# Slot tables of a graph kernel with the kind of slot outermost and the range of nodes innermost

## The chip, the cores and the metric

The kernel runs on one core of one Trainium2 chip. The metric is the device time of one execution, in microseconds. The core has a matrix engine (TensorE, PE, with a separate path PEld for loading weights), a vector engine (VectorE, DVE), a scalar engine (ScalarE, ACT), a general engine (GpSimd, POOL) and an engine that issues DMAs (SyncE, SP). DMAs are issued from SP, ACT and POOL and run on 16 DMA engines. Two kinds of memory lie on the chip: SBUF, with 128 partitions, and PSUM, into which PE writes. What is called DRAM below is the chip's large memory.

## The reference

Two layers run over the same graph of N = 32,768 nodes with 128 features and E = 524,288 directed edges (src to dst, sorted by dst).

```python
# layer 0
agg = segment_sum(x[src], dst, N)
h_local = bn(x + mlp((1 + eps) * x + agg))
h_attn = bn(x + attention(x))          # 64 blocks of 512 nodes, 8 heads
h = h_local + h_attn
x = layernorm(x + bn(h + mlp2(h)))
# layer 1, three times
attn = softmax((x @ Wq.T + bq) @ keys.T)    # 512 keys
lap = x - dinv * segment_sum(dinv[dst] * x[dst], src, N)
x = 0.5 * x + 0.5 * (attn @ values - 0.2 * lap)
# then two layer norms and a residual
```

So four sums over edges are computed: one that gathers by src and adds at dst, and three that gather by dst and add at src.

## The kernel before, in words

Nodes are cut into 256 windows of 128. An edge belongs to a pair of windows, one of its source and one of its target. The first KS = 6 edges of a pair get a regular slot; further edges of a window come in OW = 5 lists of 128, and what is left is shared by eight windows in SH = 2 lists. A window therefore has NC2 = 2 * 6 + 5 + 2 = 19 kinds of slot with 128 lanes each.

A sum over edges has two halves. In the first, `spread` multiplies the rows of a window of nodes by a pick matrix and stores the result to DRAM (`slots`), so that it can be read back by the receiving window. In the second, `Sums` fetches for each window those rows (`y_i`), gathers the 5 lists and at times the 2 shared ones with indirect DMAs on POOL (L1431), builds a one-hot matrix `oh` of 128 x 19 x 128 on DVE (`hot`, L1442), and lets PE add 19 products up in PSUM (`add`, L1455). The one-hot compares a ramp 1 to 128 with the slot table: for window i, 19 numbers per lane, each repeated over 128 columns.

The tables (slot, other, shared and row, each for "dst" and "src") depend on the edges alone and are built by the kernel itself while the attention of layer 0 runs. `prologue` is a generator: it sorts edges on DVE, moves words to their slots, transposes with PE through one PSUM bank (`turned`, L516 and L517, a copy by ACT out of that bank) and stores tables to DRAM. `attention_steps` is a list of steps written out by hand, and the last part of the program gives the generator a quota of time between steps (SHARE = 3.35 us for each place). A yield of WAIT skips places while a DMA is under way; BANK asks for a place where the PSUM bank `m`, which attention also uses, is free. The order is fixed this way, and each engine runs its own instructions in that order.

`build` handles two halves h of 128 windows each. At its end it issues on SP, in this order: the slot table of dst (L794), row of dst (L796), the regular slots of src from the tile `half` (L802), row of src (L807). The tiles of a half lie in pools that are given up and used again: `word`, in which the next half sorts (L148), lies where these tiles were. `build_more` then sorts the left-over edges: it loads `more_a` on SP (L816), first used by DVE at L236, and at its end stores the remaining 7 kinds of slot of src (L873), then other (L875) and shared (L876). Attention's own load of the next block (`xa`, L1543, read by PE at L1546) and its result (`attn_d`, L1674) go out on SP too, between these.

After attention: the spread of layer 0 (from 3,785 us), its collecting (from 4,790, when L1347 loads the slot table of dst), the MLP (6,840 to 7,075), the first spread of layer 1 (the slot table of src is loaded at 7,075), then twice collecting and spreading together (8,552 to 13,290), and the last collecting (to the end).

Before the change the slot tables have the window outermost and the 19 kinds innermost, on the chip `[128, windows, 19]` and in DRAM `(w c)`, in bfloat16.

Of the kernel before, what the change touches and what calls it, by code (L numbers as in the profile page):

```python
# [11 lines left out]
BF16 = mybir.dt.bfloat16  # L12
FP8 = mybir.dt.float8e4
AF = mybir.ActivationFunctionType
OP = mybir.AluOpType
# [4 lines left out]
P = 128  # L20
# [9 lines left out]
KS = 6  # L30
OV = 6
OW = 5
GW = 8
SH = 2
# [377 lines left out]
class Grid:  # L412
# [130 lines left out]
    def build(self, pp):  # L543
# [9 lines left out]
        with tc.tile_pool(name="gr", bufs=1) as sp:  # L553
# [13 lines left out]
            for h in range(2):  # L567
                with tc.tile_pool(name=f"gr_h{h}", bufs=1) as hp:
# [87 lines left out]
                            yield from left(over_w, 2 << b)  # L656

                    with tc.tile_pool(name=f"gr_c{h}", bufs=1) as ap:
                        slot = ap.tile([P, P, NC2], BF16, name="slot")
                        other = ap.tile([P, P, OW], I32, name="other")  # L660
                        shared = ap.tile([P, P // GW, SH], I32, name="shared")
                        keys = ap.tile([P, P], F32, name="keys")
# [14 lines left out]
                        yield one / 3  # L677
                        for t, n in ((0, 3), (3, OW - 3)):
                            yield from self.turned(pp, [fb[:, (t + j) * P:(t + j + 1) * P] for j in range(n)],
                                        slot[:, :, 2 * KS + t:2 * KS + t + n].rearrange("e w t -> e t w"))  # L680
                        nc.vector.tensor_copy(keys, fb[:, OW * P:OL])
                        yield two / 3
                        key = moved[:, :OL]
# [12 lines left out]
                        for t, n in ((0, 3), (3, OW - 3)):  # L696
                            yield from self.turned(pp, [fb[:, (t + j) * P:(t + j + 1) * P] for j in range(n)],
                                        other[:, :, t:t + n].rearrange("e w t -> e t w"))
                        yield from self.share(pp, ap, keys, fb[:, OW * P:OL], n_over, self.bad[:, at + h:at + h + 1],
                                   slot[:, :, 2 * KS + OW:].rearrange("e w t -> e t w"), shared)  # L700
                        nc.sync.dma_start(mine["shared"][:, h * P // GW * SH:(h + 1) * P // GW * SH],
                                          shared.rearrange("p g t -> p (g t)"))
                        nc.sync.dma_start(mine["other"][:, h * P * OW:(h + 1) * P * OW],
# [85 lines left out]
                        for g in range(2):  # L789
                            for r in range(0, KS, 3):  # L790
                                yield from self.turned(pp, [va[:, g, r + j, :] for j in range(3)],
                                            slot[:, :, g * KS + r:g * KS + r + 3].rearrange("d w r -> d r w"))
                                yield from self.turned(pp, [vb[:, g, r + j, :] for j in range(3)], row[:, g, r:r + 3, :])
                        nc.sync.dma_start(mine["slot"][:, h * P * NC2:(h + 1) * P * NC2],  # L794
                                          slot.rearrange("p w c -> p (w c)"))
                        nc.sync.dma_start(  # L796
                            mine["row"].rearrange("p (g h f) -> p g h f", g=2, h=2)[:, :, h, :],
                            row.rearrange("p g r w -> p g (r w)"))

                        half = ap.tile([P, NW, KS], BF16, name="half")  # L800
                        nc.scalar.copy(half.rearrange("p w r -> p (w r)"), fb)
                        nc.sync.dma_start(  # L802
                            theirs["slot"].rearrange("p (w c) -> p w c", c=NC2)[:, :, h * KS:(h + 1) * KS],
                            half)
                        row2 = ap.tile([P, 2, KS, P], BF16, name="row2")
                        nc.scalar.copy(row2, va)
                        nc.sync.dma_start(theirs["row"][:, h * Q:(h + 1) * Q],  # L807
# [1 line left out]

    def build_more(self, lane, pp):  # L810

        tc, nc, NC2, OL = self.tc, self.tc.nc, self.NC2, self.OL
        over = self.over
        with tc.tile_pool(name="mo_s", bufs=1) as sp:
            t = sp.tile([P, over.F], F32, name="more_a")
            nc.sync.dma_start(t.bitcast(I32), self.more.rearrange("p h f -> p (h f)"))  # L816
            spare = sp.tile([P, over.F], F32, name="more_b")
            yield WAIT
            yield from over.sort(sp, pp, t, spare, lane, (over.F // 2).bit_length() - 1)
        yield WAIT  # L820
        yield from over.find_windows(pp)
        L = OL + P
        with tc.tile_pool(name="mo", bufs=1) as sp:
            slot = sp.tile([P, 2, P, OW + SH], BF16, name="slot")
            other = sp.tile([P, 2, P, OW], I32, name="other")
            shared = sp.tile([P, 2, P // GW, SH], I32, name="shared")
            keys = sp.tile([P, P], F32, name="keys")
            words = []
            for h in range(2):
                words.append(sp.tile([P, L], I32, name=f"word{h}"))  # L830
                nc.gpsimd.indirect_dma_start(out=words[h], out_offset=None, in_=over.table,
                                             in_offset=bass.IndirectOffsetOnAxis(ap=over.at[:, h:h + 1], axis=0))
            yield 8 * WAIT
            for h in range(2):
                word = words[h]
                m = sp.tile([P, L], I32, name="m")
                n = sp.tile([P, L], I32, name="n")
                valid = sp.tile([P, L], F32, name="valid")
                val = sp.tile([P, L], F32, name="val")
                sz = sp.tile([P, 1], F32, name="sz")  # L840
                w = sp.tile([P, 1], F32, name="w")
                nc.vector.tensor_scalar(w, over.lane_f, float(h * P + 2), None, op0=OP.add)
                nc.vector.tensor_scalar(m, word, over.WSHIFT, None, op0=OP.logical_shift_right)
                yield L / 1000
                nc.vector.tensor_scalar(valid, m, w, None, op0=OP.is_equal, op1=OP.add, accum_out=sz)
                yield L / 1000
                nc.vector.tensor_scalar(self.bad[:, 4 + h:5 + h], sz, float(OL), None, op0=OP.is_gt)
                nc.vector.tensor_scalar(m, word, over.own, P - 1, op0=OP.logical_shift_right, op1=OP.bitwise_and)
                yield L / 1000
                nc.vector.scalar_tensor_tensor(val, m, 1.0, valid, op0=OP.add, op1=OP.mult)  # L850
                yield L / 1000
                for t, c in ((0, 3), (3, OW - 3)):
                    yield from self.turned(pp, [val[:, (t + j) * P:(t + j + 1) * P] for j in range(c)],
                                slot[:, h, :, t:t + c].rearrange("e w t -> e t w"))
                nc.vector.tensor_copy(keys, val[:, OW * P:OL])
                yield L / 1000
                nc.vector.tensor_scalar(m, word, over.OSHIFT, 2 * P - 1, op0=OP.logical_shift_right,
                                        op1=OP.bitwise_and)
                yield L / 1000
                nc.vector.tensor_scalar(m, m, 7, None, op0=OP.logical_shift_left)  # L860
                yield L / 1000
                nc.vector.tensor_scalar(n, word, over.oth, P - 1, op0=OP.logical_shift_right, op1=OP.bitwise_and)
                yield L / 1000
                nc.vector.tensor_tensor(m, m, n, OP.bitwise_or)
                yield L / 1000
                nc.vector.tensor_tensor(val, m, valid, OP.mult)
                yield L / 1000
                for t, c in ((0, 3), (3, OW - 3)):
                    yield from self.turned(pp, [val[:, (t + j) * P:(t + j + 1) * P] for j in range(c)],
                                other[:, h, :, t:t + c].rearrange("e w t -> e t w"))  # L870
                yield from self.share(pp, sp, keys, val[:, OW * P:OL], sz, self.bad[:, self.NBAD - 2 + h:self.NBAD - 1 + h],
                           slot[:, h, :, OW:].rearrange("e w t -> e t w"), shared[:, h])
            nc.sync.dma_start(self.out["src"]["slot"].rearrange("p (w c) -> p w c", c=NC2)[:, :, 2 * KS:],  # L873
                              slot.rearrange("p h w t -> p (h w) t"))
            nc.sync.dma_start(self.out["src"]["other"], other.rearrange("p h w t -> p (h w t)"))  # L875
            nc.sync.dma_start(self.out["src"]["shared"], shared.rearrange("p h g t -> p (h g t)"))  # L876

# [14 lines left out]
def tile_gnn_resnorm(ctx: ExitStack, tc: tile.TileContext, a: dict, out: bass.AP):  # L892
# [68 lines left out]
    w = {}  # L961
# [366 lines left out]
    class Exchange:  # L1328
# [14 lines left out]
            nc.sync.dma_start(self.row.rearrange("p h f -> p (h f)"), self.grid["row"])  # L1343

        def load_tables(self, pool):
            self.slot = pool.tile([P, NW, NC2], BF16, name="slot")
            nc.sync.dma_start(self.slot.rearrange("p w c -> p (w c)"), self.grid["slot"])  # L1347
            self.other = pool.tile([P, NW, OW], I32, name="other")
            nc.scalar.dma_start(self.other.rearrange("p w c -> p (w c)"), self.grid["other"])
            self.shared = pool.tile([P, NW // GW, SH], I32, name="shared")  # L1350
            nc.scalar.dma_start(self.shared.rearrange("p g c -> p (g c)"), self.grid["shared"])
# [88 lines left out]
        def hot(self, wp, i, ramp, bufs):  # L1440
            oh = wp.tile([P, NC2, P], BF16, name="oh", bufs=bufs)
            nc.vector.tensor_tensor(oh, ramp[:, None, :].to_broadcast([P, NC2, P]),  # L1442
                                    self.slot[:, i, :].unsqueeze(2).to_broadcast([P, NC2, P]), OP.is_equal)
            return oh

        def add(self, ps, oh, got, k):
# [733 lines left out]
```

## Time and profile before

| | us |
|---|---|
| Median of 3 runs | 14,449.62 (14,442.07 to 14,455.55) |
| The profiled execution: its own time | 15,348.34 |
| Its span, first to last instruction | 15,346.2 |
| PE busy | 12,388.1 (81%) |
| DVE busy | 11,407.8 (74%) |
| ACT busy | 6,684.1 (44%) |
| POOL busy | 6,062.4 (40%) |
| One-hots L1442, 1,024 of them | 2,745.6 |

The mean clock granted to PE was 0.90 of full speed. The DMA engines moved 3,603 MB in 1,733,387 packets, of which 292,786 were under 512 bytes. A busy share is an average over stages that have different limits, so a stage is read by its own waits. A line of the waits reads: engine, tile and line that waited, what it waited for, total us, times, longest us. A line of the groups reads: line, engine, operation, output and inputs with shapes, count, busy us and mean ns of one, then idle time before it and what ended it. A timeline line has start, length, engine, line, operation, output and input, count, and in brackets idle time before it. "SPq" is SP's queue of DMA issues: its length is the time of issuing, and not that of the transfer.

### The profile page before, as it was taken

The numbers are of one execution on the slowest core, as the hardware profiler recorded it, in microseconds if no ns is written. First come the engines' busy times: TensorE is split into PE (matmuls) and PEld (weight loads), VectorE is DVE, ScalarE is ACT, GpSimd is POOL, SyncE is SP. The second block draws the span as 40 slices with busy tenths as digits, with TensorE's granted clock in tenths as the row PEclk, the third lists the DMA queues.
The fourth block names the chain that finished last, engine by engine and source line by source line (L and its number), as shares of the span: only waits on it lengthen the run. The fifth ranks groups of instructions, "written<-read, shape, count | busy, mean of one in ns | idle before, by whom it ended". The sixth has DMA issues, their size and how long they took to land. (4 is left out here: it accounts for less than half of the span.)

```text
span 15346.2 us, 168164 instructions
## 1 busy us (share of the span) xinstructions
PE 12388.1 (81%) x58980; PEld 5857.4 (38%) x58982; DVE 11407.8 (74%) x16677; ACT 6684.1 (44%) x10316; POOL 6062.4 (40%) x5461
## 2 busy tenths in 40 slices
PE   8886897887886777779999798989798888755555
PEld 3222232232333333334444354444454444422222
DVE  7986996775997777777888676767566666577777
ACT  4343333334994000017888455555455555500000
POOL 0000000000003666640000577777577777566665
PEclk9887887888998888889999999999999999977777
DMA  1004004005998888877888899999899999877776
GB/s 38 10 11 13 10 10 13 13 16 50 349 347 296 259 262 263 263 228 248 304 311 308 304 367 356 364 360 361 303 366 360 359 360 361 324 250 250 248 252 223
DMA packets 1733387, 3602.99 MB, mean 235 GB/s; under 512 B 292786, under 2 KB 1069906, under 8 KB 1731378
## 3 DMA queue, kind: packets, MB, share of 16 engines
q1 hardware_dynamic: 1258736, 2936.81, 55.2%
q0 software_dynamic: 258752, 533.02, 11.8%
q10 hardware_dynamic: 215042, 122.32, 2.6%
q8 instruction: 465, 7.62, 0.2%
q14 instruction: 392, 3.21, 0.1%
HBM read 2088.45 MB, written 1503.00 MB: 234 GB/s over the span
## 5 line engine op out<-in xcount | busy, mean ns | idle before, releaser
L1431 POOL DMA_INDIRECT listed<-rows,other x5120 | 5688.1, 1111 | 4426.1 <-issue 3237.7
L1418 ACT CAST y_o<-exp 128x768 bf16<-128x768 f32 x4224 | 3238.7, 808 | 1365.2 <-PE exp L1413 867.0
L1413 PE MATMUL exp<-rows,pick 128*128 128x384 bf16 x12288 | 2784.6, 327 | 514.8 <-ACT y_o L1418 234.5
L1455 PEld LDWEIGHTS <-oh 128*128 128x128 bf16 x19456 | 2011.7, 104 | 2954.9 <-issue 1849.4
L1455 PE MATMUL seg<-y_i,oh 128*128 128x384 bf16 x12288 | 2816.1, 354 | 151.2 <-issue 141.1
L1418 DVE CAST y_o<-exp 128x768 bf16<-128x768 f32 x1920 | 1830.9, 954 | 523.1 <-PE exp L1413 427.8
L1413 PEld LDWEIGHTS <-pick 128*128 128x128 fp8e4 x12288 | 1188.0, 97 | 2217.2 <-issue 1653.0
L1455 PE MATMUL seg<-listed,oh 128*128 128x384 bf16 (+1 forms) x5120 | 1265.3, 349 | 740.3 <-issue 328.4
L1608 ACT ACTIVATE pT<-s 128x1024 f32<-128x1024 f32 x1024 | 1021.6, 1023 | 1436.2 <-PE s L1604 1434.3
L1588 DVE TENSOR_REDUCE mx<-s 128x2 f32<-128x1024 f32 x1024 | 1204.5, 1219 | 350.3 <-PE s L1582 349.8
L2007 DVE SCALAR_TENSOR_TENSOR part_i<-seg,dinv,part_i 128x128 f32<-128x128 f32 x1536 | 530.9, 346 | 1220.3 <-remote 785.7
L1442 DVE TENSOR_TENSOR oh<-ramp_p,slot 128x2432 bf16<-128x2432 f32 x512 | 1372.4, 2681 | 12.7 <-DMA slot<-slot_dst 9.4
L1442 DVE TENSOR_TENSOR oh<-iota,slot 128x2432 bf16<-128x2432 bf16 x512 | 1373.2, 2682 | 3.0 <-DMA slots<-y_o 3.0
L283 POOL DMA_INDIRECT c_r<-pivots_over,c_ix x2 | 1.9, 952 | 3244.7 <-DVE c_ix L281 3244.4
L1604 PE MATMUL s<-ql,k 32*128 32x512 f32 x4096 | 1037.3, 697 | 263.1 <-DVE mx L1588 249.8
L1066 ACT ACTIVATE ln_rs<-ln_mv,eps_c 128x4 f32<-128x4 f32 x192 | 57.1, 297 | 1930.4 <-issue 1110.2
L1944 PE MATMUL s<-pt,values 128*128 128x512 f32 x1536 | 763.6, 609 | 149.4 <-issue 131.6
L1932 PE MATMUL s<-keysT,qT 128*128 128x512 f32 x1536 | 823.5, 618 | 11.5 <-ACT pr L1045 7.4
L1582 PE MATMUL s<-k,q 32*128 32x512 f32 x4096 | 742.3, 715 | 88.2 <-DVE mx L1588 86.4
L1390 PE MATMUL row_p<-row,ident_b 128*128 128x512 bf16 x1534 | 612.7, 400 | 240.9 <-DVE pick L1401 127.1
L1615 PE MATMUL pv<-pT,vx 128*32 128x512 f32 x4096 | 700.2, 753 | 0.2 <-ACT pT L1608 0.2
L1455 PE MATMUL seg<-common,oh 128*128 128x384 bf16 (+1 forms) x2048 | 610.8, 358 | 98.9 <-issue 89.0
(393 smaller groups left out, 14261.6 us busy)
## 6 DMA issues: line engine op xcount, KB each, us to landing
slots<-y_o SPq DMA_DIRECT2D x2048, 576.0 KB
y_i<-slots SPq DMA_DIRECT2D x1024, 1152.0 KB
pick<-pick SPq DMA_DIRECT2D x1024, 192.0 KB
listed<-rows,other POOLq DMA_INDIRECT x5120
rows<-rows SPq DMA_DIRECT2D x192, 384.0 KB
part_d<-part_o SPq DMA_DIRECT2D x192, 256.0 KB
part_i<-part_d ACTq DMA_DIRECT2D x192, 256.0 KB
rows<-rows SPq DMA_DIRECT2D x64, 386.0 KB
```

The lines of the kernel that those rows point to most:

```text
L1413: nc.tensor.matmul(ps[:, j, :ROW], pick[:, o:o + P], r, start=True, stop=True)
L1418: (nc.vector.tensor_copy if to_dve else nc.scalar.copy)(dst, ps[:, :, :ROW])
L1431: nc.gpsimd.indirect_dma_start(out=g[:, k, :], out_offset=None, in_=self.table, in_offset=bass.IndirectOffsetOnAxis(ap=index[:, k:k + 1], ...
L1442: nc.vector.tensor_tensor(oh, ramp[:, None, :].to_broadcast([P, NC2, P]), self.slot[:, i, :].unsqueeze(2).to_broadcast([P, NC2, P]), OP.is ...
L1455: nc.tensor.matmul(ps[:, :n], oh[:, j, :], src, start=(k == 0), stop=(k == NC2 - 1))
L1582: nc.tensor.matmul(two[s // 2][:, s % 2, :], t["q", o][32 * s:32 * s + 32, c * P:(c + 1) * P], t["k", o][32 * s:32 * s + 32, :], start=Tru ...
L1588: nc.vector.tensor_reduce(m[:, c, 2 * i:2 * i + 2, xr[o]], st[b]["two"][i], AX.X, OP.max, negate=True)
L1604: nc.tensor.matmul(two[s // 2][:, s % 2, :], t["k", o][32 * s:32 * s + 32, c * P:(c + 1) * P], t["ql", o][32 * s:32 * s + 32, :], start=Tr ...
L1608: nc.scalar.activation(t["p", c][:, 2 * i:2 * i + 2, :], two[i], AF.Exp)
L1615: nc.tensor.matmul(t["o"][32 * s:32 * s + 32, :], t["v"][:, c, s, 2 * o:2 * o + 2, :].rearrange("p z e -> p (z e)"), t["p", c][:, s, :], s ...
L1932: nc.tensor.matmul(s, st["q"][:, c * P:(c + 1) * P], keysT, start=True, stop=True)
L1944: nc.tensor.matmul(ps, values[:, k, :], st["pt"][:, k, :], start=(k == 0), stop=(k == NCH - 1))
```

## The change

The slot tables get the 19 kinds outermost and the windows innermost: `[128, 19, windows]` on the chip and `(c w)` in DRAM. Where six or seven kinds of all windows used to be stored as runs of 6 or 7 numbers (12 and 14 bytes), they now form one run per partition; in return the two halves of the dst table, which were one run per partition each, are stored as 19 runs of 128 numbers (256 bytes). The copies out of PSUM write along the windows, `half` is copied with kinds and windows exchanged, and the one-hot reads its 19 numbers with a step of 256.

```diff
-                        slot = ap.tile([P, P, NC2], BF16, name="slot")
+                        slot = ap.tile([P, NC2, P], BF16, name="slot")
...
                             yield from self.turned(pp, [fb[:, (t + j) * P:(t + j + 1) * P] for j in range(n)],
-                                        slot[:, :, 2 * KS + t:2 * KS + t + n].rearrange("e w t -> e t w"))
+                                        slot[:, 2 * KS + t:2 * KS + t + n, :])
...
                                 yield from self.turned(pp, [va[:, g, r + j, :] for j in range(3)],
-                                            slot[:, :, g * KS + r:g * KS + r + 3].rearrange("d w r -> d r w"))
+                                            slot[:, g * KS + r:g * KS + r + 3, :])
                                 yield from self.turned(pp, [vb[:, g, r + j, :] for j in range(3)], row[:, g, r:r + 3, :])
-                        nc.sync.dma_start(mine["slot"][:, h * P * NC2:(h + 1) * P * NC2],
-                                          slot.rearrange("p w c -> p (w c)"))
+                        nc.sync.dma_start(
+                            mine["slot"].rearrange("p (c w) -> p c w", c=NC2)[:, :, h * P:(h + 1) * P], slot)
...
-                        half = ap.tile([P, NW, KS], BF16, name="half")
-                        nc.scalar.copy(half.rearrange("p w r -> p (w r)"), fb)
-                        nc.sync.dma_start(
-                            theirs["slot"].rearrange("p (w c) -> p w c", c=NC2)[:, :, h * KS:(h + 1) * KS],
-                            half)
+                        half = ap.tile([P, KS, 2, P], BF16, name="half")
+                        nc.scalar.copy(half.rearrange("p r g w -> p g r w"), vb)
+                        nc.sync.dma_start(theirs["slot"][:, h * KS * NW:(h + 1) * KS * NW],
+                                          half.rearrange("p r g w -> p (r g w)"))
...
-            slot = sp.tile([P, 2, P, OW + SH], BF16, name="slot")
+            slot = sp.tile([P, OW + SH, 2, P], BF16, name="slot")
...
-            nc.sync.dma_start(self.out["src"]["slot"].rearrange("p (w c) -> p w c", c=NC2)[:, :, 2 * KS:],
-                              slot.rearrange("p h w t -> p (h w) t"))
+            nc.sync.dma_start(self.out["src"]["slot"][:, 2 * KS * 2 * P:], slot.rearrange("p t h w -> p (t h w)"))
...
-            self.slot = pool.tile([P, NW, NC2], BF16, name="slot")
-            nc.sync.dma_start(self.slot.rearrange("p w c -> p (w c)"), self.grid["slot"])
+            self.slot = pool.tile([P, NC2, NW], BF16, name="slot")
+            nc.sync.dma_start(self.slot.rearrange("p c w -> p (c w)"), self.grid["slot"])
...
             nc.vector.tensor_tensor(oh, ramp[:, None, :].to_broadcast([P, NC2, P]),
-                                    self.slot[:, i, :].unsqueeze(2).to_broadcast([P, NC2, P]), OP.is_equal)
+                                    self.slot[:, :, i].unsqueeze(2).to_broadcast([P, NC2, P]), OP.is_equal)
```

## The prediction

> **What bounds the kernel now.** I read the page first, then the waits of the attention stage, then the SP queue's timeline around the longest of them, then the busy time of windows inside and outside. The change touches tables that are built during attention and read from 4,790 us on. The page's slices (384 us each) show that the first ten hold almost no DMA traffic, except in three that are far busier than their bytes explain; DVE dips in the same ones.
>
> ```profile
> ## 2 busy tenths in 40 slices
> ...
> DVE  7986996775997777777888676767566666577777
> ...
> DMA  1004004005998888877888899999899999877776
> GB/s 38 10 11 13 10 10 13 13 16 50 349 347 296 259 262 263 263 228 248 304 311 308 304 367 356 364 360 361 303 366 360 359 360 361 324 250 250 248 252 223
> ```
>
> The waits between 0 and 4,000 us name three long ones, each on a DMA of the SP queue:
>
> ```profile
> DVE word L148 <- DMA row_src<-row: 100.0, 1, 100.0
> ...
> DVE more_a L236 <- DMA more_a<-more: 93.2, 1, 93.2
> ...
> PE m L1546 <- DMA xa<-in_x: 86.0, 4, 63.8
> ```
>
> SP's timeline (start, length, engine, line) shows what stands in front of the first and of the third:
>
> ```profile
> 1374.69 0.51 SPq L802 DMA_DIRECT2D slot_src<-half  x1
> 1377.49 80.89 SPq L807 DMA_DIRECT2D row_src<-row  x1
> ...
> 3563.42 0.53 SPq L873 DMA_DIRECT2D slot_src<-slot  x1
> 3564.00 86.11 SPq L875 DMA_DIRECT2D other_src<-other  x1
> ```
>
> The issue at L802 looks short, but the next, a plain contiguous store, is held 81 us; the second pair (2604.34 and 2607.18) is alike with 79.21. The packets of the window 1372 to 1500, and the busy times of three stretches of 50 us, say why:
>
> ```profile
> DMA packets 33345, 1.82 MB, mean 14 GB/s; under 512 B 32832, under 2 KB 33088, under 8 KB 33344
> ```
>
> ```profile
> 1400.00:1450.00 50.00, 0.00 (x0) 0.00 (x0) 0.00 (x0) 0.00 (x0) 0.00 (x0) 0.50 1.98 5
> 2650.00:2700.00 50.00, 0.00 (x0) 0.00 (x0) 0.00 (x0) 0.00 (x0) 0.00 (x0) 0.50 1.66 40
> 3600.00:3650.00 50.00, 0.00 (x0) 0.00 (x0) 0.00 (x0) 0.00 (x0) 0.00 (x0) 0.50 1.83 5
> ```
>
> The columns after the length are PE, PEld, DVE, ACT, POOL: all zero. Nothing runs while 5 GB/s trickle out. The packets are those of the code: `half` has 128 x 256 runs of 12 bytes = 32,768, and slot_dst, row_dst, row_src 128 + 256 + 128, with 64 small completions: 33,344. Between 1375.2 and 1458.4 us (83.2) some 2,048 of them per DMA engine went by, 41 ns each. Outside the stalls attention is filled by DVE and PE (39.7 and 43.9 of 50 us between 1,300 and 1,350), so time lost here isn't made up later.
>
> **What the Trainium skill says.** "DMA: Bandwidth & Descriptors", Why a DMA increments its semaphore by 16 and not by 1: one descriptor moves one contiguous run of the last dimension; the count above agrees to the packet. The same page's Specifications: below 512 bytes the engine reads, modifies and writes; 5 GB/s fits. "Perfetto Trace Analysis", DMA Instruction — HWDGE: a DMA's recorded span ends when its descriptors are handed over, and the next may wait for the generator; so it is (0.51 then 80.89 us). "Vector Engine (DVE) Microarchitecture Reference", 5.2, has one element per cycle at 1.0417 ns plus a fixed cost: the one-hot at L1442 takes 2,681 ns for 2,432 elements, that is 2,533 + 148.
>
> **The change part by part.** All against the profiled execution, 15,348.3 us (span 15,346.2), which is 6.2% above the median of the runs, 14,449.6.
>
> *slot_src from `half` (L802, twice).* 32,768 packets become 128 of 3,072 bytes. First stall: DVE is idle from 1366.97 to 1466.92. What must still happen: ACT's copy of `half` now reads with a step of six, as its neighbour `row` does (L806, 2.93 us against 1.48), so the `row` copy ends at 1378.9 in place of 1377.5 and row_src is issued at 1379. The profile has no landing times. The nearest clean row is the load of `slot`, 1,216 KB, issued at 4789.6 and used at 4796.5: 6.9 us; for 384 KB I take 5. DVE then starts at 1384: **-83 us**. Second stall: row_src at 2608.7, more_a (1,024 KB) at 2609.2, 7 us as for `slot` plus 1 behind row_src, so DVE starts at 2617 in place of 2700.4: **-83 us**.
>
> *slot_src from `slot` in the second round (L873).* 32,768 packets of 14 bytes become 128 of 3,584. Here no table is waited for; attention's own `xa` load is caught behind the queue, issued at 3651.8. Without it, it goes out right behind aT at 3588 and lands before 3595.6, when PE comes to it. **-64 us**.
>
> *slot_dst (L794, twice).* The reverse: 128 runs of 4,864 bytes become 2,432 of 256. At the 41 ns above, 152 per engine are 6.2 us, begun at 1372.1 and done by about 1380, under the two ACT copies; at double that price it ends at 1386 and holds row_src by 2 to 3 us. Cover gone, it would cost 6 us twice. Queued behind it on SP are row_dst, slot_src, row_src, then attention's xa and attn_d.
>
> *ACT's copies out of PSUM (L517).* The attention stage by form:
>
> ```profile
> L517 ACT CAST slot<-turn 128x384 bf16<-128x384 f32 x12 | 21.5, 1794 | 10.2 <-PE turn L516 10.2
> L517 ACT CAST slot<-turn 128x256 bf16<-128x256 f32 x8 | 9.7, 1210 | 17.4 <-PE turn L516 17.4
> ...
> L517 ACT CAST row<-turn 128x384 bf16<-128x384 f32 x8 | 3.8, 480 | 4.8 <-PE turn L516 4.8
> ```
>
> `slot` is written with a step of 38 bytes, `row` in order: 1,794 against 480 ns. "SBUF — State Buffer", Specifications (16-byte cachelines), says that each access to a new line pays, which agrees. Written in order, 12 x 1.31 + 8 x 0.84 (373 ns[...]) = 22 us of ACT. The next transpose waits for the one PSUM bank `m`, but part of that lies under DVE work; bounds 0 and 22, I take half: **-11 us**.
>
> *The one-hot (L1442, 1,024 times).* Its second input now has a step of 512 bytes between 19 values in place of 2. Each is repeated 128 times, so 19 hops per instruction. The DVE page, same section, finds some 0.65 cycle per hop to a far region, an estimate of 13 ns of 2,681, hidden in the collecting stages behind POOL's gathers, PE and DMA. `vx` (L1572) hops every 64 bytes and takes 415 ns for 256 elements, 267 + 148, the same fixed part. Zero taken; 13 us if uncovered. Loads of the tables stay one run per partition.
>
> Sum: -83 - 83 - 64 - 11 = -241. The open size is what a tiny packet costs in the unprofiled runs. If the profile's extra 899 us were spread over all 1,733,387 packets, that is 0.52 ns each, 17 us for 32,768; at the other end nothing. Half, 8.5 us for each of three transfers, gives -241 + 26 = -215, and 14,449.6 - 215 = **14,235**. With no such share it is 14,209, with all of ACT's gain 14,198; with the whole share 14,260.
>
> **The rivals.** *Tiny packets are much cheaper without the profiler.* "VectorE: DVE Perf Modes", The three transpose paths, puts an element-wise 128x128 transpose by DMA at 19 times 1,309 ns, an estimate of 1.5 ns per packet against my 2.5; three transfers then cost 50 us in place of 83, and -241 + 3 x 33 = -142 gives **14,308**. For it: nothing measures unprofiled packets. Against: those writes end in another memory.
>
> *A wait takes the place of the one removed.* If 256-byte stores run at 20 us in place of 6, DVE's two restarts come some 14 us later and the gain is 215 - 28: **14,263**. Against: double the tiny price is only 12.5 us.
>
> *The end on the other side: DVE pays for every re-read.* Each value used to share its 16-byte line with seven neighbours; alone in it, each of 2,432 reads could cost more. Decision point: 215 us / 1,024 = 210 ns per one-hot, 0.09 ns per element, all on the path. At 0.2 ns it is 498 us against 215: **14,733**. Against: `vx` above, and that DVE is busy only 74% and 69% of the first and the last collecting stage (1,508 of 2,048 and 1,425 of 2,056 us).
>
> *It doesn't do what it says:* the stalls come from something else queued, and only ACT's 0 to 22 us remain: **14,439**. Against: the packet count.
>
> **How the numbers follow.** Forecast 0.60, cheaper packets 0.22, new wait 0.09, DVE re-reads 0.05, nothing removed 0.04. The range of 8 in 10 runs from 14,195 (whole ACT gain, no profiler share) to 14,325 (the cheap packets and a little less gained), which leaves out only the last two cases and the tails. About 0.2%, 29 us, is what a measurement can tell from no change. Faster by more: 0.91; within: 0.04; slower: 0.05.
>
> **What would show it.** Right: under-512-byte packets of the attention stage fall by some 93,000 (98,304 gone, 4,864 of 256 bytes come); no SP issue over a few us; DVE's waits at L148 and L236 under 20 us each and `xa` at L1546 under 25; attention's end, 3,785, near 3,544; `slot` copies near 480 ns; L1442 at 2,681. Wrong: L1442 above 2,750, a new wait of DVE on slot_dst, or attention shorter by 240 in the profile but the runs by half of that, which means the profiler made the packets dear.

## The result and the profile after

The kernel after takes 14,203.28 us (14,183.13 to 14,207.12) against 14,445.85 for the kernel before in the same measurement: a ratio of 0.9828, with a 95% interval of 0.9816 to 0.9839, that is 243 us less (233 to 266). The prediction said 14,235 and faster. The profiled execution of the kernel after has a span of 14,199.4 us and a time of its own of 14,201.3, so here the profile and the runs agree.

The page of the kernel after, slices and packets. A slice is now 355 us, not 384:

```profile
DVE  7998998776998888877888677777677777778888
...
DMA  1000000000999999977888899999999999988887
...
DMA packets 1640075, 3602.99 MB, mean 254 GB/s; under 512 B 199346, under 2 KB 976466, under 8 KB 1638066
```

The two 4s and the 5 in the DMA row of the first ten slices are gone; in the same slices DVE goes from 6, 6 and 5 tenths to 8, 8 and 6. The bytes are the same. Packets under 512 bytes fell from 292,786 to 199,346, by 93,440: 98,304 tiny ones gone, 4,864 of 256 bytes come, as foretold.

The waits of the kernel after between 0 and 4,000 us (engine, tile and line that waited, what for, total us, times, longest), where before they had 100.0, 93.2 and 86.0:

```profile
DVE word L148 <- DMA row_src<-row: 12.4, 1, 12.4
...
DVE more_a L236 <- DMA more_a<-more: 7.6, 1, 7.6
...
PE m L1544 <- DMA xa<-in_x: 19.2, 1, 19.2
```

The three differences are -87.6, -85.6 and -66.8, together -240.0. The third line adds up several waits; the single one of 63.8 us is gone, and what is left is the first load of the program. SP's timeline shows why (start, length):

```profile
1369.54 0.32 SPq L802 DMA_DIRECT2D slot_src<-half  x1
1372.32 0.33 SPq L806 DMA_DIRECT2D row_src<-row  x1
...
3374.17 0.42 SPq L873 DMA_DIRECT2D other_src<-other  x1
```

The issue behind `half` takes 0.33 us where it took 80.89, and the one behind the last `slot` 0.42 where it took 86.11. The stretches of 50 us after the two places are full (PE, PEld, DVE, ACT, POOL as busy us):

```profile
1400.00:1450.00 50.00, 45.36 (x222) 14.30 (x222) 46.04 (x45) 19.95 (x24) 0.00 (x0) 0.86 0.04 11
2650.00:2700.00 50.00, 40.34 (x209) 15.12 (x211) 39.01 (x40) 19.43 (x24) 0.00 (x0) 0.86 0.00 1
```

ACT's copies by form in the attention stage, with the mean in ns behind the busy time, and the one-hots of the first and the last collecting from the page:

```profile
L517 ACT CAST slot<-turn 128x384 bf16<-128x384 f32 x12 | 5.8, 482 | 10.0 <-PE turn L516 10.0
L517 ACT CAST slot<-turn 128x256 bf16<-128x256 f32 x8 | 3.0, 375 | 17.6 <-PE turn L516 17.6
```

```profile
L1440 DVE TENSOR_TENSOR oh<-ramp_p,slot 128x2432 bf16<-128x2432 f32 x512 | 1372.3, 2681 | 12.7 <-DMA slot<-slot_dst 9.4
```

`slot` now costs what `row` costs (482 ns for 384 elements, was 1,794), and the one-hot stayed at 2,681 although its 19 numbers lie 512 bytes apart; the other 512 took 2,683 ns, before 2,682.

Attention ends, where the rows for the first spread are loaded, at 3,529.2 us instead of 3,785.5 in the first profile of the kernel before: -256.3, of which the three waits are -240.0. That profile took 899 us longer than the runs. Against a second one, below, which took about as long as they do, attention is 250.0 us shorter, the three waits 227.8, and 22 us are left.

### The profile page after: what moved, and what is told of

Same layout as the page of the kernel before. It is cut to its first block, busy times and chain, and to the rows that moved or that the text cites. A ratio compares the mean times of both kernels' runs of the same rounds, so it can differ in the third digit from the quotient of the medians.

```text
span 14199.4 us, 168166 instructions
## 1 busy us (share of the span) xinstructions
PE 12173.8 (86%) x58982; PEld 5828.9 (41%) x58982; DVE 11413.1 (80%) x16677; ACT 6658.1 (47%) x10316; POOL 6079.5 (43%) x5461
## 2 busy tenths in 40 slices
DMA packets 1640075, 3602.99 MB, mean 254 GB/s; under 512 B 199346, under 2 KB 976466, under 8 KB 1638066
## 5 line engine op out<-in xcount | busy, mean ns | idle before, releaser
L1453 PE MATMUL seg<-y_i,oh 128*128 128x384 bf16 x12288 | 2745.0, 349 | 9.3 <-DMA y_i<-slots 9.3
L1440 DVE TENSOR_TENSOR oh<-ramp_p,slot 128x2432 bf16<-128x2432 f32 x512 | 1372.3, 2681 | 12.7 <-DMA slot<-slot_dst 9.4
L1440 DVE TENSOR_TENSOR oh<-iota,slot 128x2432 bf16<-128x2432 bf16 x512 | 1373.7, 2683 | 3.0 <-DMA slots<-y_o 3.0
L1942 PE MATMUL s<-pt,values 128*128 128x512 f32 x1536 | 750.6, 600 | 10.8 <-ACT pt L1937 10.6
```

Source lines behind the costliest of these rows:

```text
L1453: nc.tensor.matmul(ps[:, :n], oh[:, j, :], src, start=(k == 0), stop=(k == NC2 - 1))
L1942: nc.tensor.matmul(ps, values[:, k, :], st["pt"][:, k, :], start=(k == 0), stop=(k == NCH - 1))
```

## The experiments

My theory: the 98,304 tiny pieces on SP's queue cost three waits of 67 to 88 us, because what is queued behind them on SP is issued late; ACT's copies add about 10 us, DVE's one-hots nothing. Rivals: it is the dst tables and ACT's copies that gain; it is the scattered places in DRAM rather than the number of pieces; it is the DMA engines, full of pieces, or a tile in memory that can't be used again yet, and not the queue. And one part of the prediction was open from the start: the 899 us by which the first profiled execution was longer than the runs.

### The kernel before, profiled again

> The kernel before, unchanged, looked at once more. If the 899 us by which the first profiled execution was longer than the runs belong to that execution, this one takes about 14,450 us, attention still ends near 3,785 us and the first collecting stage takes about 1,720 us in place of 2,048. If the profiler itself costs them, the span is again near 15,346.

Its time was 14,469.41 us, its span 14,467.5. The same waits in it:

```profile
DVE word L148 <- DMA row_src<-row: 96.9, 1, 96.9
DVE more_a L236 <- DMA more_a<-more: 89.2, 1, 89.2
...
PE m L1546 <- DMA xa<-in_x: 80.9, 3, 59.7
```

They are within 3 to 5 us of those of the 899 us longer execution. Attention ends at 3,779.2 instead of 3,785.5. The three collecting stages, in the order of the program, differ by 333, 290 and 259 us, 882 together, and the spans by 879, so that is all of it. The groups of POOL's gathers say the same (busy, mean ns, idle before). In the first profile of the kernel before:

```profile
L1431 POOL DMA_INDIRECT listed<-rows,other x5120 | 5688.1, 1111 | 4426.1 <-issue 3237.7 <-PE seg L1455 486.5 <-remote 433.8
```

and in this one:

```profile
L1431 POOL DMA_INDIRECT listed<-rows,other x5120 | 5745.6, 1122 | 3541.2 <-issue 3164.7 <-PE seg L1455 163.4 <-DMA listed<-rows,other 68.9
```

The gathers themselves take as long; the idle time in front of them is 885 us shorter. So the extra time had nothing to do with the tiny packets. It isn't the profiler's either: the kernel before took 15,355 us run after run in the measurement of two kernels below (all three stores on ACT's queue with `half` among the constants, and `half` in pieces of 64 bytes), and 15,251 in that of two others (32 bytes, and `row2` in 64 bytes too). All five profiles of such long executions have 4,342 to 4,436 us of idle time before these gathers, the nine others 3,521 to 3,555. The record names a chip for each measurement of the experiments: 4 and 5 where the kernel before took 14,452 and 14,422 us, 15 and 10 where it took 15,355 and 15,251; for the first profile it names none. The chip, or what else ran on it, is the nearest suspect. What makes the gathers wait was not found.

### The src table alone, and the dst table alone

In the first kernel only the src table has the new order, in the second only the dst table. Each keeps the old order and the old stores for the other, and the one-hot reads either.

```diff
+            self.by_kind = key == "src"
...
-            self.slot = pool.tile([P, NW, NC2], BF16, name="slot")
-            nc.sync.dma_start(self.slot.rearrange("p w c -> p (w c)"), self.grid["slot"])
+            shape = [P, NC2, NW] if self.by_kind else [P, NW, NC2]
+            self.slot = pool.tile(shape, BF16, name="slot")
+            nc.sync.dma_start(self.slot.rearrange("p a b -> p (a b)"), self.grid["slot"])
```

> Only the src tables in the new order: the 98,304 packets of 12 and 14 bytes go, the dst table, its copies out of PSUM and its store stay as before. Theory (three stalls from the tiny packets): 85 + 85 + 65 = 235 us less than before, near 14,211. Rival (a large part comes from ACT's copies in order, most of which belong to dst): less than 200 gained.

> Only the dst table in the new order: ACT's copies in order and 256-byte runs in its store, the tiny packets of src stay. Theory: the three stalls stay and some 8 us are gained (4 before each half's end), near 14,438, at most 20. Rival (the store in 256-byte runs or the one-hot with a step of 512 bytes costs something): 0 to 30 us slower than before.

Src alone: 14,229.25 us, ratio 0.9846 (0.9831 to 0.9862), that is -223 against the 14,452 of the kernel before. Dst alone: 14,439.49, ratio 0.9992 (0.9983 to 1.0), that is -13, with an interval from -25 to 0. The waits with src alone, and then with dst alone:

```profile
DVE word L148 <- DMA row_src<-row: 14.6, 1, 14.6
...
DVE more_a L236 <- DMA more_a<-more: 7.9, 1, 7.9
```

```profile
DVE word L148 <- DMA row_src<-row: 97.1, 1, 97.1
DVE more_a L236 <- DMA more_a<-more: 89.6, 1, 89.6
```

All the tiny pieces belong to src, and so does nearly all of the gain. Dst brings most of ACT's gain (the two forms of L517 took 8.1 + 6.1 = 14.2 us of ACT in this kernel, 31.2 before) at the price of 4,864 pieces of 256 bytes, and the time hardly sees either. -223 and -13 make -236 of the -243 measured together. The profiles add up less well: attention ends at 3,553.4 us with src alone and at 3,777.9 with dst alone, which is 225.7 and 1.3 us earlier than in the second profile of the kernel before, where both together bring 250.0.

### The same long runs, cut into pieces again

The kernel after, but with `half` padded on the chip so that it must be read in pieces of 16 bytes. In DRAM it is written in order, as in the kernel after. 24,576 pieces for each half; the third store, of the left-over edges, keeps its long runs.

```diff
-                        half = ap.tile([P, KS, 2, P], BF16, name="half")
-                        nc.scalar.copy(half.rearrange("p r g w -> p g r w"), vb)
+                        half = ap.tile([P, KS, 2, P // 8, 10], BF16, name="half")
+                        for g in range(2):
+                            nc.scalar.copy(half[:, :, g, :, :8],
+                                           vb[:, g].rearrange("p r (a b) -> p r a b", b=8))
...
+                            half.rearrange("p r g a b -> p (r g a) b")[:, :, :8])
```

> The changed kernel, but half lies on the chip in pieces of 8 numbers with gaps, so that its store reads 24,576 pieces of 16 bytes per half and writes one contiguous run per partition in DRAM. If the number of pieces costs, wherever they are: 24,576 at 2.54 ns are 62 us, so two stalls of some 60 us come back, near 14,320. If it is the scattered small writes in DRAM that cost: no stall, 14,200 to 14,225.

14,368.49 us, ratio 0.9941 (0.9926 to 0.9957): 165 us over the kernel after. Two of the three waits are back, and SP's issue behind the store is held again:

```profile
DVE word L148 <- DMA row_src<-row: 96.4, 1, 96.4
DVE more_a L236 <- DMA more_a<-more: 91.9, 1, 91.9
```

```profile
1375.41 73.02 SPq L809 DMA_DIRECT2D row_src<-row  x1
```

So the order of the places in DRAM is not needed for the wait; pieces are enough. 73.02 us / 24,576 is 3.0 ns for each, dearer than the 2.5 ns (83.2 us / 33,344) of the 12-byte ones. By the count alone I had expected 62 us.

### The same tiny pieces, on another queue

The kernel before with its pieces as they were, but the three slot_src stores issued by ACT.

```diff
-                        nc.sync.dma_start(
+                        nc.scalar.dma_start(
                             theirs["slot"].rearrange("p (w c) -> p w c", c=NC2)[:, :, h * KS:(h + 1) * KS],
                             half)
...
-            nc.sync.dma_start(self.out["src"]["slot"].rearrange("p (w c) -> p w c", c=NC2)[:, :, 2 * KS:],
+            nc.scalar.dma_start(self.out["src"]["slot"].rearrange("p (w c) -> p w c", c=NC2)[:, :, 2 * KS:],
```

> The kernel before with all its tiny packets, but the three stores of slot_src are issued on ACT's queue, which attention doesn't use otherwise. Theory (what costs is to stand in front of others on SP's queue): more_a, other and xa go out at once, the second and third stall go (85 + 60), the first stays, since the tile half must be read before word may lie there; near 14,300. Rival (the tiny packets occupy the 16 DMA engines or one shared generator of descriptors, whatever the queue): all three stay, 14,430 to 14,460.

14,333.82 us, ratio 0.9936 (0.9918 to 0.9953): -88, with an interval from -118 to -68. The expected 14,300 rested on 85 + 60 = 145 us less. The waits, and a window in the middle of the second store:

```profile
DVE word L148 <- DMA slot_src<-half: 91.5, 1, 91.5
DVE more_a L236 <- DMA more_a<-more: 25.9, 1, 25.9
...
PE m L1546 <- DMA xa<-in_x: 35.8, 2, 19.1
```

```profile
2650.00:2675.00 25.00, 22.70 (x121) 7.86 (x122) 23.84 (x23) 12.44 (x15) 0.00 (x0) 0.93 1.89 6
```

6 GB/s still trickle out, yet DVE is busy for 23.84 of 25 us. The tiny pieces don't stop the core; the queue did, at the second and the third place. Not all of it went, though: the second wait keeps 25.9 us where the kernel after has 7.6, and the third 16.7 besides the program's first load of 19.1. The three are 153 us together, 114 less than in the kernel before. At the first the wait stayed, and now has another name: not row_src but slot_src. `word` of the next half lies where `half` was, and DVE may not write there before the store has read it. The profile of the kernel before named row_src because that came last.

### Without the memory wait: a miss, and what it showed

Two more kernels put `half` into a tile of its own in a pool that lives through both halves: one on top of the store on ACT's queue, the other with the store on SP as before (and `row2` in a place of its own too).

```diff
+            halves = [sp.tile([P, NW, KS], BF16, name=f"half{h}") for h in range(2)]
...
-                        half = ap.tile([P, NW, KS], BF16, name="half")
+                        half = halves[h]
```

> As act_q, and half lies in memory of its own, so that word doesn't wait for its store. Theory: all three stalls go though all 98,304 tiny packets are still sent; near 14,215 plus what row_src, more_a and xa lose by sharing the engines with them, 5 to 20 us each: 14,220 to 14,270. Rival (engines or generator): stays at 14,430 to 14,460.

> The kernel before, with half and row2 in memory of their own and all stores on SP as before. If the wait named in the profile (word for row_src) is the cause of the first stall, it goes whole: 85 us less, near 14,365. If SP's queue is: attention runs on until it needs the next xa, which stands behind the tiny packets, and only 20 to 40 us of the first stall go; the second and third stay; near 14,420.

On ACT's queue: 14,353.45 us, ratio 0.9938 (0.9918 to 0.9958), no better than without the tiles of its own, where 14,220 to 14,270 had been expected. The waits of this kernel:

```profile
DVE flip_i L233 <- DMA slot_src<-half: 79.9, 1, 79.9
DVE word L148 <- DMA row_src<-row: 33.2, 1, 33.2
```

The first wait shrank to a third as foreseen, but the pool's place is used again by the tiles of `build_more`, so the same wait turned up at the second place.

On SP's queue: 14,398.31 us, ratio 0.9978 (0.9969 to 0.9988), that is 17 to 45 us less. The waits of this one, on DVE and then on PE:

```profile
DVE flip_i L233 <- DMA row_src<-row: 80.4, 1, 80.4
...
DVE word L148 <- ACT row L808: 10.6, 1, 10.6
...
PE m L1548 <- DMA xa<-in_x: 113.9, 4, 52.8
```

DVE's wait at L148 is down to 10.6, and PE waits for attention's load of the next block in its place (113.9 where it was 80.9, with one wait more). At L233 `flip_i` waits for the old place, as in the other kernel. Of the 86 us that the named wait lost, the time shows 17 to 45, in line with the second of the two expectations: what is behind it in the queue is late next.

### Both at once, in a place that nothing else uses

Store on ACT's queue, and `half` in the pool of the constants, which is never given up.

```diff
+        self.halves = [pool.tile([P, NW, KS], BF16, name=f"half{h}") for h in range(2)]
...
-                        half = ap.tile([P, NW, KS], BF16, name="half")
+                        half = self.halves[h]
```

> The kernel before, with its 98,304 twelve-byte pieces as they were, but the three slot_src stores issued on ACT's queue and the copies they are read from in places of their own that nothing else ever uses. Theory (the stalls were the queue behind the store and the memory that the store was still reading, not the pieces as such): all three stalls shrink, to about 33, 20-26 and 16 us, and the kernel gains about 170 us: 14,255-14,290 against a before of 14,440, ratio about 0.988. Rival (the DMA engines, full of tiny pieces, hold back the loads that attention and the build wait for): a stall of 70 us or more stays somewhere and the gain is that of the run with ACT's queue alone, about 92 us, ratio about 0.994.

Here the kernel before took 15,354.88 us and this one 15,217.54: ratio 0.9906 (0.9889 to 0.9922), that is -137, between -170 and -120. So it gained more than with the queue alone; the 170 I had expected lies at the very edge of the interval. The waits, and a window in the middle of the second store:

```profile
DVE word L148 <- DMA row_src<-row: 34.9, 1, 34.9
DVE more_a L236 <- DMA more_a<-more: 24.4, 1, 24.4
...
PE m L1547 <- DMA xa<-in_x: 51.3, 4, 19.4
```

```profile
2600.00:2625.00 25.00, 22.24 (x127) 7.65 (x128) 24.86 (x24) 13.03 (x16) 0.00 (x0) 1.00 1.96 5
```

All 98,304 tiny pieces are still sent. The first two waits are as expected (33 and 20 to 26), the third, without the first load of 19.4, is 32 where 16 had been expected. The three are 111 us together, 267 in the second profile of the kernel before: -156, and attention ends at 3,619.7 instead of 3,779.2. That divides the cost of the pieces in two. Some 156 us of it came from what stood behind the store, in SP's queue and in the memory it was reading. Attention still ends 90 us later than in the kernel after (3,529.2), and 71 of these are in the same three waits: 34.9 against 12.4, 24.4 against 7.6, 51.3 against 19.2. Here row_src was issued at 1381.2, in 0.32 us, and DVE went on only at 1404.8, 23.6 us later; in the kernel after it is 2.6. The 384 KB of this store can be seen in the traffic in steps of 2.5 us from 1372 on:

```profile
GB/s 0 198 212 12 5 4 5 10 31 50 48 40 9 5 5 4 5 5 5 4 4 5 5 4 6 5 5 5 5 5 14 34 62 93 31 1 0 0 0 0
```

Only from about 1389 to 1402 do they stand out of the trickle of tiny pieces, at 10 to 50 GB/s. So with SP's queue free the plain store was itself slow while the pieces were under way. I take it that it shared the DMA engines with them, which no run here shows apart from other causes; only fewer pieces took this part away.

### How short is too short

The kernel after, with `half` cut as above into 6,144 pieces of 64 bytes, then into 12,288 of 32 bytes; and with `half` and `row2` both in pieces of 64 bytes, 12,288 together. The edits are those of the 16-byte kernel with `P // 32, 34` and b=32 for 64 bytes, `P // 16, 18` and b=16 for 32 bytes. The third store keeps its long runs in all of them.

> The kernel after, with the half of the table that has 8,192 places' slots read from the chip in 6,144 pieces of 64 bytes instead of 1,536 or fewer long runs. Theory (a price per piece, 3.0 ns as with 16-byte pieces, whatever its length): 18 us for each of these stores, the first two stalls some 10-15 us longer than in the kernel after, the kernel about 14,235, ratio 0.9858. Rival (64 bytes are as good as 256): no stall grows, about 14,203. Other rival (the price grows with length): 14,260 or more.

> The kernel after, with each `half` stored in 12,288 pieces of 32 bytes. In the run with 64 bytes a piece took 0.73 ns; with 16 bytes it took 3.0 ns, but only after some 2,500 pieces that went at about 0.6. Theory (the length decides: pieces shorter than 64 bytes are dear): 2.5-3 ns each, 31-37 us per store, row_src's issue held for some 20-30 us, the two stalls together some 40-50 us longer than in the kernel after. Rival (the number waiting in the queue decides, dear beyond some thousands, whatever the length): also dear here, from about the 2,500th piece on; then the run with as many pieces of 64 bytes is dear as well. Other rival (only 16 bytes and less are dear): 9 us per store, nothing to be seen in the time.

> The kernel after, with both `half` and the src rows (row2) stored in 6,144 pieces of 64 bytes each, so 12,288 of them one behind the other, as many as in the run with 32-byte pieces. Theory (the length decides): 0.73 ns each all through, 9 us for the two, at 88 GB/s; the two stalls some 5 us longer each than in the kernel after, time within 15 us of it. Rival (the number waiting decides): GB/s falls off within the two stores, a stall of 25 us and more.

Each row is set against the kernel before of its own measurement.

| pieces of `half` | ratio to before | us saved | wait at L148 | wait at L236 |
|---|---|---|---|---|
| 3,072 bytes (the kernel after) | 0.9828 (0.9816 to 0.9839) | 243 | 12.4 | 7.6 |
| 64 bytes | 0.9846 (0.9830 to 0.9863) | 229 | 15.0 | 9.7 |
| 64 bytes, `row2` too | 0.9854 (0.9838 to 0.9871) | 228 | 19.5 | 13.1 |
| 32 bytes | 0.9832 (0.9815 to 0.9848) | 249 | 19.9 | 13.4 |
| 16 bytes | 0.9941 (0.9926 to 0.9957) | 84 | 96.4 | 91.9 |

GB/s in steps of half a us from 1372 on, with pieces of 16 bytes and then of 32. The stretch up to about the fifth number is other tables:

```profile
GB/s 219 340 323 185 32 26 22 7 11 5 5 7 8 5 3 4 5 4 4 8 5 3 5 6 7 5 7 4 4 2 4 3 5 6 5 4 7 4 5 2
```

```profile
GB/s 216 219 282 372 233 83 49 50 49 50 49 50 49 50 49 50 49 50 48 49 123 148 92 111 358 25 18 0 0 0 0 0 0 0 0 0 0 0 0 0
```

With 32 bytes the store runs at a steady 49 to 50 GB/s, which is 0.65 ns for each piece, and is over before the tenth us. With 64 bytes it is 88 to 89 GB/s, 0.73 ns, also with 12,288 pieces. With 16 bytes it begins at 32 to 22 GB/s (0.5 to 0.7 ns) for one and a half us, some 2,500 pieces, and then falls to about 5 (3 ns). The 12-byte pieces of the kernel before begin in the same way, at 20, 20 and 18 GB/s (0.6 ns) for one and a half us, some 2,400 pieces. Both of my theories fell: not all pieces below 64 bytes are dear, and it is not the number either, since 12,288 pieces of 32 bytes run through without falling off. What holds is the third: the price per piece jumps between 16 and 32 bytes, by a factor of 4 to 5. The times of the first four rows can hardly be told apart, and their two waits differ by 13 us together at most: in the two stores of `half`, runs of 32 bytes won as much as the runs of 3,072.

"DMA: Bandwidth & Descriptors" of the Trainium skill says, in How a descriptor splits into AXI transactions, that the unit in which a descriptor's bytes travel is 32 bytes. The jump lies there, but no run here shows that it is the cause: these kernels also differ in how far apart the pieces lie on the chip (20, 36 and 68 bytes), and two pieces of 16 bytes lie in each 32 bytes of DRAM. The same page's limit of 512 bytes (Specifications), which the prediction cited, is not what made these stores dear: runs of 32, 64 and 256 bytes are below it too.

### Copies and stores issued earlier

The kernel after, with the copies and stores of `half` and `row2` put ahead of the last transposes, so that the wait of 12.4 us at L148 might go.

```diff
+                        half = ap.tile([P, KS, 2, P], BF16, name="half")
+                        nc.scalar.copy(half.rearrange("p r g w -> p g r w"), vb)
+                        nc.sync.dma_start(theirs["slot"][:, h * KS * NW:(h + 1) * KS * NW],
+                                          half.rearrange("p r g w -> p (r g w)"))
...
                         for g in range(2):
                             for r in range(0, KS, 3):
```

> The changed kernel with the copies and stores of half and row2 placed ahead of the last transposes. DVE's remaining waits of 12 and 8 us shrink by some 5 us each: 0 to 15 us less than the changed kernel, 14,190 to 14,205, hardly to be told from it by time; the profile shows the waits.

14,213.81 us, ratio 0.9844 (0.9826 to 0.9862), and attention ends at 3,529.6 instead of 3,529.2: nothing gained. DVE still waits at L148, for the table that is now last:

```profile
DVE word L148 <- DMA row_dst<-row: 9.4, 1, 9.4
```

No kernel here beat the kernel after by more than the intervals.

## Why the prediction was right, step by step

The likeliest case came true: measured 14,203, foretold 14,235, range 14,195 to 14,325.

- **First and second stall, -83 each.** -84.5 and -81.6 against the second profile of the kernel before, -87.6 and -85.6 against the first, from which the prediction was worked out. At the first, row_src was issued 9.8 us after DVE fell idle (1362.5 to 1372.3) where I had put 12, and was there 2.6 us later where I took 5; at the second, DVE idled 7.6 us where the sum left 9.8. The mechanism, SP's queue, is shown by the stores moved to ACT's queue: the second wait fell from 89.2 to 25.9. It was not whole: the first stall was held as well by the memory that the store was reading (91.5 us with the queue free), which the profile of before could not show because the wait took the name of what came last; and with both out of the way the waits still hold 71 us more than in the kernel after. The number came out all the same, since the change takes the pieces away and with them whatever they held, and that part is luck. The prediction also took the held issue as the next one waiting for the generator of descriptors. With the store on ACT's queue, SP's issue of row_src takes 0.32 us although the same pieces are being sent, so what holds the issue is SP's own queue.
- **Third stall, -64.** -61.7 against the second profile, -66.8 against the first. Attention's load goes out behind a 0.42 us issue.
- **slot_dst in 256-byte runs, nothing.** Right: 608 KB at about 217 GB/s take 2.9 us, begun some 7 us before row_src is issued, 19 ns for a piece on each engine, where I had put 41 ns and 6.2 us. Equal prices for all short pieces was the wrong assumption here, but it did no harm to the sum.
- **ACT's copies, -11 of a possible 22.** ACT's time fell by 22.4 us in the two forms, as worked out (the 1,794 ns of before are a mean: two of the 12 copies are src's, with a step of 14 bytes in place of 38). How much of it arrives is not shown. Without its three waits attention would end at 3,512 us in the second profile of the kernel before, at 3,511 with src alone, at 3,510 with dst alone and at 3,490 in the kernel after. So the 22 us that are left beside the waits come only with both tables, while dst alone, with 17 of ACT's 22 us, has almost none of it in its profile, and in its time -13 with an interval that reaches 0. By the same count the five kernels derived from the kernel after lie between 3,471 and 3,497, so one profile tells it to some 25 us only. What these 22 us are stays open.
- **The one-hot, nothing.** 2,681 ns before and after in one form, 2,682 and 2,683 in the other.
- **The profiler's share, +26.** This is the term that failed. I had spread the 899 us over all packets and taken half of the share that falls on three transfers. They lay in the idle time before POOL's gathers, in the three collecting stages, and the second profile of the kernel before didn't have them. Without the term the sum is 14,209, 6 us from what was measured. That it is so close is in part luck: attention is 250 us shorter in the profiles of usual length, 9 more than the 241 of the sum, and the runs show 243 (233 to 266).
- **Rivals.** Cheaper packets (14,308): no, the runs themselves gained 243 us where 50 us for a transfer would have given 142, and the waits of 96.9 and 89.2 stand in an execution that took as long as the runs. A new wait on the 256-byte stores (14,263): no, 2.9 us. DVE pays for re-reads: no. Nothing removed: no.

## What to carry to other kernels

A store cut into tens of thousands of pieces of 12 to 16 bytes costs some 80 us here, and those who pay are the ones queued behind it or waiting for the memory that it reads: look at the issue *after* the store, not at the store's own. Lay the table out so that a piece has 32 bytes or more, the shortest that was cheap here; another queue alone won 88 us of 243, another place for the source some 30, both 137. Before a wait is taken away, ask who stands next in the same queue or the same memory, for the time usually goes there.

## What was not expected of the hardware

- The price of a piece jumps: 3.0 ns at 16 bytes, 2.5 at 12, but 0.65 at 32 and 0.73 at 64, and 1.2 at 256 (608 KB at 217 GB/s). Pieces were dear where only the places on the chip had gaps (16 bytes) as well as where those in DRAM had (12 bytes).
- About the first 2,500 tiny pieces go at 0.5 to 0.7 ns, with 16 bytes as with 12, and only then does the store slow to 3. What fills up there stays open.
- A wait names the last of its releasers: row_src in the kernel before, slot_src as soon as row_src no longer had to queue.
